# One decay-zero scan over both channel tiles in the first chunks of a Mamba, attention and expert kernel

## The chip, the cores and the metric

The kernel runs on one core of one Trainium2 chip. The metric is the device time of one launch in microseconds. Before the change the median of three runs is 3574.44 us (3572.05 to 3581.58). Engine names: PE is the matrix engine, DVE the vector engine, ACT the scalar engine with the activation tables, POOL the general engine that here issues accumulating transfers and small copies, SP the engine that only issues transfers.

## The reference

Eight samples of 256 channels by 1024 tokens go through two layers. The first layer is a Mamba block and a feed-forward block, the second is attention over the 1024 tokens of a sample and a mixture of experts. The change touches only the scan of the Mamba block:

```python
def step(h, inputs):
    dt_t, B_t, C_t, x_t = inputs
    dA = jnp.exp(dt_t[..., None] * A)
    h = dA * h + (dt_t * x_t)[..., None] * B_t[:, None, :]
    y = jnp.einsum('bds,bs->bd', h, C_t)
    return (h, y)
...
h0 = jnp.zeros((B, d_inner, d_state), x.dtype)
_, ys = jax.lax.scan(step, h0, seq)
```

There are 512 inner channels (`d_inner`) and 16 states (`d_state`), so a sample has 512 x 16 recurrences of 1024 tokens, each of which starts at zero. All is in float32.

## The kernel before

**Tiles.** Channels lie on the 128 partitions, tokens along the free dimension. The 512 inner channels are four tiles of 128; two tiles form a half (`h` is 0 or 1, and `q` is the tile within it). A sample is cut into two chunks of 512 tokens, so there are 16 chunks, numbered from 0. An even chunk is the first of its sample and starts from the state zero; an odd one is the second and starts from what the first left in `state`.

**A step.** A chunk has 32 steps, one for each state `s` and half `h`; a global step number is `g`. A step does this:

- `decay(g, q)`, L595, on ACT: `da = exp(dt * -A)` for the tile `q`, 128 x 512, into one of four rotating buffers `da`.
- `inputs(g)`, L605, on DVE: `hb = xd * B`, 128 x 1024, both tiles of the half in one instruction. `B` and `C` come as `bc`, which SP loads ahead.
- `scan(g, q)`, L616, on DVE: the recurrence along 512 tokens, in place in `hb[:, q, :]`, one instruction for each tile. Its start value is the constant 0 in an even chunk and a column of `state` in an odd one. In an even chunk, after the second scan, POOL copies the last column of both tiles to `state` (L629).
- `sums(g)`, L631, on DVE: `hb = hb * C`, in place; then POOL issues a transfer that adds `hb` to the chunk's accumulator `dx` (L639).

**The loop** (L1688 to L1715) goes over all 512 steps. For each it emits scan 0, then decay 0 of the step two ahead, scan 1, then decay 1 of the step two ahead, the inputs of the next step, and this step's sums. The decay of two steps ahead takes the buffer that the scan just emitted has read.

**What else is woven in.** After every one of these DVE instructions `advance()` (L1607) runs. It holds a clock of its own, kept by costs written into the kernel (L104 to L115: a scan is charged 0.16 us and 2.08 ns for each column, other vector work 0.16 us and 1.04 ns), and emits the pieces of other streams that the clock says are ready: the prologue of the next chunk (`prologue`, L462: normalization, projection, convolution, `dt`), the gate (`gate_part`, L642), the epilogue of the chunk before (`epilogue`, L674: output projection and feed-forward), attention (L1075) and the experts (L1298). Urgencies are at L1588. Attention of a sample runs in 32 units, each of four score matmuls, exponentials on ACT, and eight sums on PE. Where the clock finds PE idle, `keep_warm` (L1593) emits a matmul with zero weights (`warm`, or into an open attention sum, `num`). So the order of the instructions on each engine is fixed when the kernel is built, and the clock decides it. The prologue of chunk i + 1 starts at the step `FRONT[i]` of chunk i (L252), the gate at `GATE[i]` (L253). The prologue ends with the products of `xm` and `dt` (L574), for which the accumulating transfers into `dt` must have landed; the steps of the next chunk can't begin before (L1700).

**The end.** After the last step the last chunk's epilogue, the attention of the last sample and its experts remain, with what is left of the sample before.

Nearly all instructions are recorded at one line (L100, or L95 for transfers), since a helper issues them; in the views they are told apart by the names of their tiles.

Of the kernel before, what the change touches and what calls it, by code (L numbers as in the profile page):

```python
# [9 lines left out]
F32 = mybir.dt.float32  # L10
BF16 = mybir.dt.bfloat16
I32 = mybir.dt.int32
AF = mybir.ActivationFunctionType
ALU = mybir.AluOpType
# [3 lines left out]
P = 128  # L18
B, C, L = 8, 256, 1024
KC = C // P  # L20
CH = 512
NCH = L // CH
# [6 lines left out]
NSTEP = NHALF * NS  # L29
# [25 lines left out]
def hybrid_kernel(ctx: ExitStack, tc: tile.TileContext, a: dict, out: bass.AP):  # L55
# [6 lines left out]
    class Model:  # L62
# [3 lines left out]
        t = end = moved = 0.0  # L66
# [50 lines left out]
    act, vec = Queue(nc.scalar, act_cost), Queue(nc.vector, vec_cost)  # L117
# [51 lines left out]
    zero_c = const.tile([P, 1], F32, name="zero_c")  # L169
# [12 lines left out]
    neg_a = const.tile([P, ND * NS], F32, name="neg_a")  # L182
# [21 lines left out]
    state = const.tile([P, NS, ND], F32, name="state")  # L204
# [255 lines left out]
    chunk = {}  # L460
# [119 lines left out]
    das, bcs, hbs = {}, {}, {}  # L580

    def load_bc(n):
        i, s = divmod(n, NS)
        bc = work_pool.tile([P, 2, CH], F32, name=f"bc_{n}", tag="bc", bufs=AHEAD + 1)
        landed = sp.dma_start(
            bc, chunk[i]["bc_d"][s].partition_broadcast(P)
        )
        bcs[n] = (bc, landed)

    def place(g):  # L590
        i, k = divmod(g, NSTEP)
        s, h = divmod(k, NHALF)
        return i, s, h

    def decay(g, q):  # L595
        i, s, h = place(g)
        da = work_pool.tile([P, CH], F32, name=f"da_{g}_{q}", tag="da", bufs=4)
        n = (2 * h + q) * NS + s
        act.activation(da, chunk[i]["dt"][h][:, q, :], AF.Exp, scale=neg_a[:, n : n + 1])
        das[g, q] = (da, act.at)  # L600
        if q and s == NS - 1:
            model.end = act.at
            t4.put(chunk[i]["dt"][h])

    def inputs(g):  # L605

        i, s, h = place(g)
        hb = hbs[g] = h4.now(f"hb_{g}")
        bc, landed = bcs[g // NHALF]
        vec.at = max(vec.at, landed)  # L610
        xd = chunk[i]["xd"][h]
        vec.tensor_tensor(hb, xd, bc[:, 0, :].unsqueeze(1).to_broadcast([P, 2, CH]), ALU.mult)
        if s == NS - 1:
            t4.put(xd)

    def scan(g, q):  # L616

        i, s, h = place(g)
        c = i % NCH
        hb = hbs[g]  # L620
        d = 2 * h + q
        da, done = das.pop((g, q))
        vec.at = max(vec.at, done)
        vec.tensor_tensor_scan(
            hb[:, q, :], da, hb[:, q, :], 0.0 if c == 0 else state[:, s, d : d + 1],
            ALU.mult, ALU.add,
        )
        if q and c < NCH - 1:
            pool.tensor_copy(state[:, s, 2 * h : 2 * h + 2], hb[:, :, CH - 1])  # L629

    def sums(g):  # L631

        i, s, h = place(g)
        me = chunk[i]
        bc, _ = bcs[g // NHALF] if h < NHALF - 1 else bcs.pop(g // NHALF)
        hb = hbs.pop(g)
        vec.tensor_tensor(hb, hb, bc[:, 1, :].unsqueeze(1).to_broadcast([P, 2, CH]), ALU.mult)
        model.t = vec.at
        me["landed", h] = pool.dma_start(out=me["acc", h], in_=hb, accum_op=ALU.add)  # L639
        h4.put(hb, at=me["landed", h])  # L640

    def gate_part(i):  # L642

        me = chunk[i]
        mem = Owner(t4, 3, 2)
        xn = yield from mem.take(f"xz_{i}")
        yield sp.dma_start(xn, me["xn_d"])
        sz, ps = [], None
        for d in range(ND + 1):
            if d:  # L650
                h, q = divmod(d - 1, 2)
                act.activation(
                    sz[h][:, q, :], ps, AF.Identity, bias=b_in[:, ND + d - 1 : ND + d]
                )
                banks.put(ps)
            if d < ND:
                if d % 2 == 0:
                    sz.append((yield from mem.take(f"sz_{i}_{d // 2}")))
                ps = yield from banks.take(f"z_{i}_{d}")
                for k in range(KC):  # L660
                    pe.matmul(
                        ps, w_in[:, k, DI + d * P : DI + (d + 1) * P], xn[:, k, :],
                        start=(k == 0), stop=(k == KC - 1),
                    )
                yield
        mem.put(xn)
        for t in sz:
            act.activation(t, t, AF.Silu)
        lnexp()
        mem.end()  # L670
        yield
        me["sz"] = sz
# [887 lines left out]
    with tc.tile_pool(name="work", bufs=1) as work_pool:  # L1560

        def tagged(tag, n):
            return Slots(
                lambda nm, k: work_pool.tile([P, 2, CH], F32, name=nm, tag=f"{tag}_{k}"), n
            )

        t4, h4, pt4 = tagged("t4", T4), tagged("h4", H4), tagged("pt", PT)
        for b in range(B):
            for m, nm in ((x1_d, "x1_d"), (t_d, "t_d"), (xf_d, "xf_d")):
                m[b] = dram.tile([NCH, P, KC, CH], F32, name=f"{nm}_{b}", tag=f"{nm}_{b}")  # L1570
# [16 lines left out]
        due, done = [], set()  # L1587
        URGENT = {"a": 0, "p": 1, "g": 2, "e": 2, "o": 3, "s": 4, "x": 5, "y": 5}  # L1588

        def start(stream, key, at=0.0):  # L1590
            due.append([at, URGENT[key[0]], len(done) + len(due), stream, key])
# [15 lines left out]
        def advance():  # L1607


            while True:  # L1610
                model.t = min(model.t + TICK, vec.at)
                for d in sorted(due, key=lambda d: d[1:3]):
                    while d in due and d[0] <= model.t + 0.05:
                        if d[1] > 2 and max(pe.at, act.at) > model.t + LAG:
                            break
                        model.end = model.t
                        try:
                            at = next(d[3])
                        except StopIteration:
                            due.remove(d)  # L1620
                            done.add(d[4])
                            break
                        if at == POLL:
                            break
                        d[0] = (model.end if at is None else at) + 0.1
                keep_warm()
                if model.t >= vec.at:
                    break

        def idle(t):  # L1630

            vec.at += t
            advance()
# [48 lines left out]
        nsteps = B * NCH * NSTEP  # L1682
        for n in range(AHEAD):
            load_bc(n)
        for n in range(4):
            decay(n // 2, n % 2)
        inputs(0)
        for now in range(nsteps):  # L1688
            i, k = divmod(now, NSTEP)
            if i + 1 < B * NCH and k == FRONT[i]:  # L1690
                start(prologue(i + 1), ("p", i + 1), model.t)
            if k == GATE[i]:
                start(gate_part(i), ("g", i), model.t)
            n = now // NHALF + AHEAD
            if now % NHALF == 0 and n < B * NCH * NS:
                while "bc_d" not in chunk.get(n // NS, {}):
                    idle(0.5)
                load_bc(n)
            if now + 2 < nsteps:
                while "dt" not in chunk.get((now + 2) // NSTEP, {}):  # L1700
                    idle(0.5)
            for q in range(2):
                scan(now, q)
                advance()
                if now + 2 < nsteps:
                    decay(now + 2, q)
            if now + 1 < nsteps:
                while not h4.free:
                    idle(0.5)
                inputs(now + 1)  # L1710
                advance()
            sums(now)
            if k == NSTEP - 1:
                start(epilogue(i), ("e", i), model.t)
            advance()  # L1715
# [13 lines left out]
    with tc.If(large != 0):  # L1729
# [21 lines left out]
        with tc.tile_pool(name="moe", bufs=1) as pl:  # L1751
# [99 lines left out]
            for b in range(B):  # L1851
# [8 lines left out]
                hb = pl.tile([P, 2, NF], F32, name=f"hb_{b}", tag="mhb", bufs=2)  # L1860
# [24 lines left out]
                for c in range(NCH):  # L1885
                    tok = slice(c * CH, (c + 1) * CH)
                    n = f"{b}_{c}"
                    h = pl.tile([P, 2, NF, CH], F32, name=f"mh_{n}", tag="mh", bufs=2)
# [9 lines left out]
                    r = pl.tile([P, KC, CH], F32, name=f"mr_{n}", tag="mr", bufs=2)  # L1898
# [80 lines left out]
```

## Time and profile before

| | |
|---|---|
| median of the runs | 3574.44 us |
| the profiled execution | 3582.58 us, its span 3580.8 us |
| scans with start value 0 (even chunks) | 512, mean 1210 ns |
| scans with a start value from `state` (odd chunks) | 512, mean 1269 ns |
| products `hb<-xm,bc` and `hb<-hb,bc` | 512 each, mean 1204 and 1221 ns |
| decays on ACT | 1024, mean 718 ns |
| copies of the last column on POOL | 256, mean 900 ns |
| granted clock of PE | 0.949 on average |

The page gives each engine's busy time, the span in 40 slices with a digit for tenths, the chain of work that ended last, and groups of instructions. A group's line has its engine, operation, tiles (out, then in), shapes, count, busy time in us and mean length in ns, then the idle time of the engine just before them and what ended it. The recorded lengths of neighbours on one engine can overlap: their sum is more than the time from the first start to the last end. A view in stretches gives, for each of a list of windows, the busy time of each engine in us with the number of instructions; PEclk is the granted clock.

### The profile page before, as it was taken

Reading aid. Unit: us, or ns where it says so; the run is one execution under the profiler, and the core shown is the slowest. Engines: PE = TensorE matmul, PEld = TensorE weight load, DVE = VectorE, ACT = ScalarE, POOL = GpSimd, SP = SyncE. Lnnn points to the kernel's source line nnn. Section 1 sums busy time; section 2 is a strip of 40 time slices with the busy share of each in tenths; the row PEclk is TensorE's granted clock in tenths of the full one; section 3 lists DMA queues with packets and bytes.
Section 4 is the critical chain, followed back from the end, with each engine's and each line's share of the span. In section 5 each row is a group of like instructions: output and inputs, shape, how many; then the busy total and the mean of one; then the engine's idle time right before and its main releaser. Section 6 shows DMA issues by size and latency. Waiting matters only on the chain.

```text
span 3580.8 us, 40009 instructions
## 1 busy us (share of the span) xinstructions
PE 3235.4 (90%) x14383; PEld 1419.1 (40%) x14383; DVE 3023.1 (84%) x3308; ACT 2468.9 (69%) x3539; POOL 947.5 (26%) x1052
## 2 busy tenths in 40 slices
PE   8876859998999999999999999898999999999997
PEld 5544344333443334343433344333434343335334
DVE  4879999999999999999999999989999999971021
ACT  4463737686687866797778777796778777854644
POOL 0233123312342224322331234223332233211010
PEclk9778989999999999999999999999999999999999
DMA  4667787778788878987787878897788878861120
GB/s 119 162 139 169 175 180 176 165 176 191 193 195 205 181 167 201 209 197 177 189 206 169 207 191 196 186 206 165 175 206 177 197 196 189 204 139 65 38 72 16
DMA packets 187329, 605.66 MB, mean 169 GB/s; under 512 B 25440, under 2 KB 36320, under 8 KB 187120
## 3 DMA queue, kind: packets, MB, share of 16 engines
q0 software_dynamic: 103392, 364.44, 52.4%
q1 hardware_dynamic: 83728, 238.57, 20.6%
q8 instruction: 115, 1.88, 0.2%
q14 instruction: 94, 0.77, 0.1%
HBM read 238.55 MB, written 62.39 MB: 84 GB/s over the span
## 4 chain that ended last, share of the span: by engine, by line
PE 36%; DVE 33%; issue 11%; ACT 7%; DMA 7%; POOL 5%; POOLq 0%; DVEq 0%; SPq 0%; ACTq 0%
DVE hb L100 25%; PE re L100 4%; PE he L100 3%; POOL state L100 3%; PE num L100 3%; PE sc L100 3%; PE warm L100 3%; PE fh L100 3%; DVE xm L100 3%; DMA dx<-hb 2%; PE facc L100 2%; PE den L100 2%; PE qkp L100 2%; ACT L100 2%; DMA dt<-u 2%
## 5 line engine op out<-in xcount | busy, mean ns | idle before, releaser
L100 ACT ACTIVATE da<-dt,neg_a 128x512 f32<-128x512 f32 x1024 | 720.1, 718 | 486.8 <-DVE hb L100 471.0
L95 POOL DMA_DIRECT2D dx<-hb x512 | 442.8, 867 | 1618.4 <-DVE hb L100 1351.2
L100 DVE TENSOR_TENSOR hb<-hb,bc 128x1024 f32<-128x1024 f32 x512 | 625.2, 1221 | 51.5 <-POOL state L100 20.8
L100 DVE TENSOR_TENSOR_SCAN hb<-da,state,hb 128x512 f32<-128x512 f32 x512 | 632.7, 1269 | 7.7 <-ACT da L100 7.7
L100 DVE TENSOR_TENSOR hb<-xm,bc 128x1024 f32<-128x1024 f32 x512 | 616.5, 1204 | 8.1 <-DMA dx<-hb 8.0
L100 DVE TENSOR_TENSOR_SCAN hb<-da,hb 128x512 f32<-128x512 f32 x512 | 603.0, 1210 | 1.0 <-ACT da L100 0.9
L100 ACT ACTIVATE pt<-sc 128x1024 f32<-128x1024 f32 x512 | 493.8, 1016 | 99.2 <-PE sc L100 98.9
L100 PE MATMUL warm<-mean_c,zero_c 128*128 128x256 f32 x1398 | 417.3, 427 | 46.9 <-ACT dt L100 10.0
L100 PE MATMUL sc<-qk,qk 32*128 32x512 f32 x2048 | 344.4, 652 | 24.0 <-ACT pt L100 17.9
L100 POOL COPY state<-hb 128x2 f32<-128x2 f32 x256 | 230.3, 900 | 436.7 <-DVE hb L100 424.6
L100 PEld LDWEIGHTS warm<-mean_c,zero_c 128*128 128x128 f32 x1398 | 263.4, 205 | 207.1 <-PE warm L100 78.1
L100 PE MATMUL num<-pt,v 128*32 128x512 f32 x2048 | 282.4, 621 | 41.1 <-DVE ot L100 40.9
L100 PE MATMUL den<-pt,ecb 128*32 128x512 f32 x2048 | 277.3, 610 | 0.0
L100 PE MATMUL facc<-fh,w 128*128 128x512 f32 x512 | 231.5, 600 | 4.9 <-ACT re L100 2.8
L100 PE MATMUL fh<-x_f,w 128*128 128x512 f32 x480 | 227.2, 606 | 3.0 <-DVE xn L100 1.7
L100 PE MATMUL he<-xe,g 128*128 128x512 f32 x448 | 217.5, 613 | 5.9 <-ACT xp L100 3.7
L100 ACT ACT_TABLE_LOAD x169 | 216.8, 1283 | 7.6 <-PE var_a L100 4.0
L100 PE MATMUL re<-he,g 128*128 128x512 f32 x472 | 217.0, 607 | 2.6 <-ACT pt L100 2.1
L100 PEld LDWEIGHTS sc<-qk,qk 32*128 32x128 f32 x2048 | 105.7, 186 | 216.0 <-ACT pt L100 108.2
L100 PE MATMUL mo<-sz,w_out 128*128 128x512 f32 x256 | 120.9, 616 | 55.9 <-DVE sz L100 55.9
L100 DVE SCALAR_TENSOR_TENSOR xm<-xp,vecs,xm 128x512 f32<-128x512 f32 x192 | 143.3, 747 | 8.4 <-ACT xm L100 3.9
L100 PEld LDWEIGHTS facc<-fh,w 128*128 128x128 f32 x512 | 95.6, 191 | 125.0 <-issue 114.4
(349 smaller groups left out, 4107.9 us busy)
## 6 DMA issues: line engine op xcount, KB each, us to landing
dx<-hb POOLq DMA_DIRECT2D x512, 512.0 KB
bc<-bc_d SPq DMA_DIRECT2D x256, 512.0 KB
dt<-e POOLq DMA_DIRECT2D x32, 512.0 KB
dt<-u POOLq DMA_DIRECT2D x32, 512.0 KB
xe<-xf_d SPq DMA_DIRECT2D x28, 512.0 KB
xn<-in_x SPq DMA_DIRECT2D x16, 512.0 KB
xn_d<-xn SPq DMA_DIRECT2D x16, 512.0 KB
xz<-xn_d SPq DMA_DIRECT2D x16, 512.0 KB
```

What stands on the lines that cost most here:

```text
L95: f(*args, **kw)
L100: return f(*args, **kw)
```

## The change

In even chunks one scan now covers both tiles of the half: 1024 columns, the first tile's 512 tokens and then the second's. For the second tile's recurrence to start at zero, the decay at its first token is zero. Three things go with it:

- The four rotating decay buffers become one tile `da_all`, 2 (step parity) x 2 (tile) x 512, so that both tiles' decays are adjacent.
- For the second tile in even chunks the decay leaves out the first column and computes 511. The zero is written there by a copy on ACT, for the first two steps of each even chunk only (one for each parity); nothing overwrites it until the next odd chunk.
- In even chunks both decays of the step two ahead are emitted after the wide scan. In odd chunks the order is as it was.

```diff
     def decay(g, q):
         i, s, h = place(g)
-        da = work_pool.tile([P, CH], F32, name=f"da_{g}_{q}", tag="da", bufs=4)
+        da = da_all[:, g % 2, q, :]
         n = (2 * h + q) * NS + s
-        act.activation(da, chunk[i]["dt"][h][:, q, :], AF.Exp, scale=neg_a[:, n : n + 1])
-        das[g, q] = (da, act.at)
+        skip = 1 if q and i % NCH == 0 else 0
+        if skip and g % NSTEP < 2:
+            act.copy(da[:, :1], zero_c)
+        act.activation(
+            da[:, skip:], chunk[i]["dt"][h][:, q, skip:], AF.Exp, scale=neg_a[:, n : n + 1]
+        )
+        das[g, q] = act.at
...
-        da, done = das.pop((g, q))
+        done = das.pop((g, q))
         vec.at = max(vec.at, done)
-        vec.tensor_tensor_scan(
-            hb[:, q, :], da, hb[:, q, :], 0.0 if c == 0 else state[:, s, d : d + 1],
-            ALU.mult, ALU.add,
-        )
+        if c == 0:
+            if q:
+                both = hb.rearrange("p a t -> p (a t)")
+                vec.tensor_tensor_scan(
+                    both, da_all[:, g % 2].rearrange("p a t -> p (a t)"), both, 0.0,
+                    ALU.mult, ALU.add,
+                )
+        else:
+            vec.tensor_tensor_scan(
+                hb[:, q, :], da_all[:, g % 2, q, :], hb[:, q, :], state[:, s, d : d + 1],
+                ALU.mult, ALU.add,
+            )
...
+        da_all = work_pool.tile([P, 2, 2, CH], F32, name="da_all", tag="da")
...
                 scan(now, q)
                 advance()
-                if now + 2 < nsteps:
-                    decay(now + 2, q)
+                if now + 2 < nsteps and (q or i % NCH):
+                    for r in range(0 if i % NCH == 0 else q, q + 1):
+                        decay(now + 2, r)
```

## The prediction

> **What bounds the kernel now.** I read the page's busy shares, then the 40 slices, the costliest groups, the waits of DVE, the busy time in stretches cut at each chunk's first scan, and last the timelines of DVE in a first chunk and of PE at the end.
>
> ```profile
> PE 3235.4 (90%) x14383; PEld 1419.1 (40%) x14383; DVE 3023.1 (84%) x3308; ACT 2468.9 (69%) x3539; POOL 947.5 (26%) x1052
> ...
> PE   8876859998999999999999999898999999999997
> ...
> DVE  4879999999999999999999999989999999971021
> ...
> PE 36%; DVE 33%; issue 11%; ACT 7%; DMA 7%; POOL 5%; POOLq 0%; DVEq 0%; SPq 0%; ACTq 0%
> ...
> L100 DVE TENSOR_TENSOR_SCAN hb<-da,state,hb 128x512 f32<-128x512 f32 x512 | 632.7, 1269 | 7.7 <-ACT da L100 7.7
> ...
> L100 DVE TENSOR_TENSOR_SCAN hb<-da,hb 128x512 f32<-128x512 f32 x512 | 603.0, 1210 | 1.0 <-ACT da L100 0.9
> L100 ACT ACTIVATE pt<-sc 128x1024 f32<-128x1024 f32 x512 | 493.8, 1016 | 99.2 <-PE sc L100 98.9
> L100 PE MATMUL warm<-mean_c,zero_c 128*128 128x256 f32 x1398 | 417.3, 427 | 46.9 <-ACT dt L100 10.0
> ```
>
> Two engines are full at once. DVE is at nine tenths until slice 36 and then nearly empty; PE stays full for the rest. So there are two regimes: the scan stretch (first scan at 93 us, last one over at 3186 us, by the scans' own records) and a tail of 395 us in which PE works alone. The second scan group is the one the change touches: 512 scans of 512 columns whose start value is the constant 0. Before them DVE waits for a decay 1.0 us in all, so they are bound by DVE itself.
>
> ```profile
> core 0: us, PE busy (x) PEld busy (x) DVE busy (x) ACT busy (x) POOL busy (x), PEclk, DMA share, GB/s
> ...
> 865.00:1063.00 198.00, 179.80 (x580) 82.14 (x580) 183.07 (x208) 135.38 (x194) 77.79 (x84) 0.97 0.84 194
> 1063.00:1249.00 186.00, 173.28 (x885) 67.45 (x883) 181.03 (x175) 151.25 (x213) 38.33 (x44) 0.97 0.87 194
> ...
> 3186.00:3581.00 395.00, 365.62 (x1749) 159.59 (x1748) 66.50 (x159) 188.33 (x238) 30.21 (x32) 0.98 0.17 47
> ```
>
> The first two rows are a first chunk (of sample 2) and the second chunk behind it: DVE busy 92 and 97%, PE 91 and 93%. The last is the tail: PE 93%, DVE 17%.
>
> ```profile
> 549.81 2.33 DVE L100 TENSOR_TENSOR_SCAN hb<-da,hb 128x512 f32<-128x512 f32 x2
> 552.06 1.20 DVE L100 TENSOR_TENSOR hb<-xm,bc 128x1024 f32<-128x1024 f32 x1
> 553.34 1.23 DVE L100 TENSOR_TENSOR hb<-hb,bc 128x1024 f32<-128x1024 f32 x1
> 554.48 0.28 DVE L100 SCALAR_TENSOR_TENSOR sq_a<-var_a,sq_a 128x128 f32<-128x128 f32 x1
> ```
>
> A step of a first chunk: from the pair's start to the next start is 552.06 - 549.81 = 2.25 us. The recorded lengths (1.21 each) overlap, so starts count, not lengths. By the single records the second scan starts 1.134 us after the first, and the product behind it 1.116 us after the second.
>
> [...] No run yet shows a scan of 1024 columns.
>
> **Part by part.**
>
> *256 pairs become 256 scans.* The streaming stays; one fixed term per pair goes. [...] Bounds: [...] if the wide scan streams no better than the pair, 0. All eight first chunks hold these, and DVE has no cover there.
>
> *The wide scan waits for both decays.* Before, half q's decay was needed only by scan q. Both are now issued behind the wide scan, since they overwrite buffers that it reads. Room: from its end to the scan two steps on lie four products and a scan, 4 x 1.12 + 2.2 = 6.7 us, against two decays of 0.72. What is queued on ACT ahead can be a Gelu block (four of about 1 us and two table loads of 1.28 us: 6.6 us), which just about fits. Cost: 0 taken, at most 1 us for three blocks in each of 8 chunks, 24 us. Behind a late scan stand the products, POOL's state copy and its DMA.
>
> *ACT.* 256 decays of 511 columns instead of 512, with an odd first word: nothing by the row (0.72 us at either length)[...]. 16 copies of one column at 0.18 us (the row of copies of three columns): 3 us on ACT, hidden. POOL's state copies and all DMA issues are as many as before; they follow the scan as before, and nothing is moved past SP's queue.
>
> *The order.* The planner in the kernel charges each merged pair 0.16 us less, so everything that it weaves between the steps moves. In the emitted order of both programs I weighted PE's matmuls with their spacing in the trace (0.86 us for a full 512-column product, 3.15 us for an attention unit of 4 scores and 8 sums):
>
> - Before the last scan PE has 18 us less real work, ACT about 14 us less, DVE 9 small instructions less (about 4 us).
> - Behind the last scan stand 42 attention units instead of 37, and 20 small normalization matmuls more. The trace fits: 292 score records / 8 = 36.5 units lie behind the last scan.
> - The second chunks get heavier: chunks 5 and 7 each take 14 us more PE work, the first chunks before them less.
> - 70 more keep-warm matmuls (821 to 891) are emitted.
> - The last product of the prologues of chunks 5, 11 and 13 moves from step 29 to steps 26, 26 and 27 of the chunk before. That relieves a wait for the landing of dt, 2.3 us at 1052 us (chunk 5's).
>
> ```profile
> 3189.18 1.37 PE L100 MATMUL sc<-qk,qk 32*128 32x512 f32 x8
> 3190.48 1.07 PE L100 MATMUL num<-pt,v 128*32 128x512 f32 x8
> 3191.36 1.04 PE L100 MATMUL den<-pt,ecb 128*32 128x512 f32 x8
> 3192.34 1.20 PE L100 MATMUL sc<-qk,qk 32*128 32x512 f32 x8
> ```
>
> These are units in the tail, 3.16 us apart with no gap: five more cost 16 us unless they fill holes. From 3186 to 3400 us PE is idle or warming only about 15 us, and the new order emits as many warm matmuls there, so I let them fill nothing; the small matmuls add 1 to 2 us.
>
> *Sum.* Scan stretch: -17 (merge) - 4 (moved DVE work) - 2 (dt) = -23 us. Tail: +17 us. Net -6 us. The profiled execution took 3582.58 us (span 3580.8 and 1.8 around it), 8.1 above the median of the runs, 3574.44; I put the difference on the median: 3568 us.
>
> **Rivals.**
>
> *A, the likeliest (0.50):* the scans' gain arrives and the tail takes most of it back: 3568, between 3558 and 3580 by the bounds above. For it: both engines are full, and PE's real work is unchanged. What isn't saved in PE's holes isn't saved.
>
> *B, the tail pays little (0.25):* the five units fill PE's waits in the last epilogue (9 us warm, 2 idle between 3186 and 3285), and the second chunks carry their added PE work in their own holes (20 to 26 us each). Then -23 + 5 = -18: 3556. Against it: the unchanged count of warm matmuls.
>
> *C, second chunks run over (0.20):* in them the last prologue product stays at step 29, so the next chunk's scans wait for it, and PE gets up to 14 us more ahead of it. Chunk 7 has 170 us of real PE work (its matmul records less the warm ones) in 193; with 184 it would be at 95%, above the 93% that the fullest stretch reaches. If the prologue ends 5 us late in each of the five chunks 5, 7, 9, 11 and 13: +25 - 6 = +19: 3593. It decides once the waits for dt in these chunks, 2 to 4 us now where there are any, grow by more than 3 us each. The 70 added warm matmuls, 0.43 us each, 30 us of PE time, speak for holes of this kind.
>
> *D, no saving (0.05):* the wide scan takes as long as the pair: +17 on A's sum, 3585.
>
> **How the numbers follow.** A measurement of this kernel can tell about 0.3%, 11 us, from no change: under 3563.7 is faster, over 3585.2 slower. A gives faster 0.17, same 0.32, slower 0.01; B faster 0.23, same 0.02; C slower 0.20; D same 0.02, slower 0.03. Sum: faster 0.40, same 0.36, slower 0.24. The range takes B's middle and C's: 3548 to 3593. A's own is 3558 to 3580.
>
> **What would show it.** A group of 256 scans of 1024 columns, 2.26 to 2.28 us by record and 2.18 to 2.20 us from start to start: the merge's step. Start to start of 2.25: D. Last scan's end some 20 us earlier and a tail of about 410 us: A; a tail of under 402: B. Waits for dt or for prologue steps that grow in odd chunks, and a stretch no shorter than before: C. DVE's wait for decays above 10 us in the new group would make the decay step wrong. I am wrong altogether if the end moves by more than 25 us either way.

## The result, and the profile after

The changed kernel takes 3631.35 us (median of four runs, 3625.80 to 3634.05). Before, in the same comparison, it is 3573.24 us (four runs, 3567.18 to 3581.58). The ratio of the means is 1.0159, with a 95% interval of 1.0134 to 1.0184: the change makes the kernel 1.6% slower, and the time lies above the range of the prediction. The profiled execution took 3625.80 us with a span of 3624.0, 43.2 us more than the span of before.

The page of the changed kernel, first the busy shares, then the rows of PE and DVE over 40 slices, then three groups (busy us, mean ns | idle before):

```profile
PE 3276.6 (90%) x14523; PEld 1444.1 (40%) x14523; DVE 3008.8 (83%) x3052; ACT 2464.3 (68%) x3555; POOL 939.8 (26%) x1052
...
PE   8866959998889999999899999999999998999997
...
DVE  4979999999999899998999999979999799951021
...
L100 DVE TENSOR_TENSOR_SCAN hb<-da_all,state,hb 128x512 f32<-128x512 f32 x512 | 631.3, 1270 | 2.3 <-ACT da_all L100 2.3
...
L100 DVE TENSOR_TENSOR_SCAN hb<-da_all,hb 128x1024 f32<-128x1024 f32 x256 | 584.7, 2284 | 2.1 <-ACT da_all L100 2.1
...
L100 PE MATMUL warm<-mean_c,zero_c 128*128 128x256 f32 x1482 | 450.3, 432 | 35.6 <-ACT dt L100 9.0
```

The change does what it says: 256 scans of 1024 columns stand where 512 of 512 stood, and DVE waits for their decays 2.1 us in all. DVE is busy 14.3 us less than before (3023.1 to 3008.8), yet the span is longer. PE is busy 41 us more, but without the matmuls of zero weights its work is about the same (2777 us before, 2774 after): the rest is keep-warm work, 84 more of these records in the group above and 140 more in all, 1690 to 1830. A matmul leaves two records here (the four score matmuls of a unit stand as `x8` in the timelines), so these are 70 matmuls more. Neither engine got more of the reference's work to do: DVE waits more, and PE fills more time with zero weights.

The wide scan itself in DVE's timeline (start, length, instruction), at the place shown of before:

```profile
554.64 1.22 DVE L100 TENSOR_TENSOR hb<-hb,bc 128x1024 f32<-128x1024 f32 x1
555.78 2.29 DVE L100 TENSOR_TENSOR_SCAN hb<-da_all,hb 128x1024 f32<-128x1024 f32 x1
557.98 1.20 DVE L100 TENSOR_TENSOR hb<-xm,bc 128x1024 f32<-128x1024 f32 x1
```

From its start to the next start are 557.98 - 555.78 = 2.20 us, against 2.25 for the pair. Over the 161 such cases in the trace the mean is 2.201: 49 ns saved, 256 x 0.049 = 12.5 us.

**Where the 43 us are.** I cut the DVE records of both traces at the first scan of each chunk, and summed the idle time ahead of each instruction. "Work" is the stretch from the first scan to the end of the last, less these waits. The last column is experiment 6, which comes below.

| us | before | after | experiment 6 |
|---|---|---|---|
| first scan | 93.3 | 96.3 | 96.5 |
| DVE's work in the stretch | 2911.8 | 2889.4 | 2886.1 |
| DVE's waits in even chunks | 107.7 | 107.3 | 109.7 |
| DVE's waits in odd chunks | 73.6 | 114.2 | 67.8 |
| tail | 394.3 | 416.8 | 417.0 |
| span | 3580.8 | 3624.0 | 3577.1 |

DVE does 22.4 us less in the stretch, 12.5 of it by the merge; the rest moved out of it. Then it waits 40.5 us more in the odd chunks, whose steps the change leaves as they were, and the tail is 22.5 us longer. Of the waits in odd chunks, those ahead of the prologue's instructions (`xm`, `e`, `xn`, `sq_a`, `xp`) grow from 14.5 to 40.7 us, and those ahead of other streams' instructions from 43.3 to 67.5; those ahead of the steps' own shrink from 15.8 to 5.9. Sorted by what ended them (waits over 0.15 us), those for ACT grow most, from 21.5 to 50.9 us; those for PE grow from 26.8 to 36.6 and those for transfers from 19.9 to 22.1. By chunk the prologue's waits are:

| odd chunk | 1 | 3 | 5 | 7 | 9 | 11 | 13 | 15 |
|---|---|---|---|---|---|---|---|---|
| before, us | 0.3 | 0.4 | 2.4 | 3.9 | 0.4 | 1.0 | 6.0 | 0 |
| after, us | 0.3 | 0.5 | 9.6 | 10.5 | 6.3 | 3.4 | 10.1 | 0 |

The busy time by stretch of the changed kernel, for chunks 4, 5 and 7 and the tail (the columns' names are in the first line):

```profile
core 0: us, PE busy (x) PEld busy (x) DVE busy (x) ACT busy (x) POOL busy (x), PEclk, DMA share, GB/s
868.00:1068.00 200.00, 170.07 (x508) 80.33 (x500) 180.59 (x175) 123.89 (x183) 76.59 (x83) 0.92 0.80 187
1068.00:1265.00 197.00, 186.91 (x946) 71.90 (x942) 181.24 (x175) 161.40 (x227) 39.15 (x45) 0.97 0.84 187
...
1458.00:1666.00 208.00, 201.35 (x962) 78.23 (x960) 181.25 (x174) 170.01 (x237) 49.81 (x51) 0.98 0.81 185
3207.00:3624.00 417.00, 382.48 (x1888) 165.59 (x1884) 70.68 (x168) 200.37 (x254) 31.03 (x33) 0.98 0.18 49
```

and chunk 7 before:

```profile
1444.00:1637.00 193.00, 184.20 (x898) 72.44 (x894) 181.42 (x174) 158.34 (x222) 50.50 (x52) 1.00 0.89 202
```

Chunk 5 had 186 us before with the same 181 us of DVE work; now it takes 197, so DVE's share falls from 97 to 92%. Chunk 7 grew from 193 to 208 us, and PE is busy 97% of it, 95% before. In chunk 4 PE is busy less than before (170 against 180 us), and the chunk is no shorter. So PE's load went from a first chunk, which gained nothing by it, into second chunks that were nearly full. Without the matmuls of zero weights PE is busy 862 us of the five odd chunks from 5 to 13 before and 900 after; together these chunks last 978 us before and 1005 after.

The end of chunk 7 shows one prologue that runs late, here with a wait for a transfer; it is the longest of its kind, not the commonest kind. First before, the last `e` and the two products `xm<-xm,dt` that close the prologue, from DVE's timeline:

```profile
1599.40 1.21 DVE L100 SCALAR_TENSOR_TENSOR e<-u,e 128x1024 f32<-128x1024 f32 x1
...
1615.99 1.22 DVE L100 TENSOR_TENSOR xm<-xm,dt 128x1024 f32<-128x1024 f32 x1
...
1625.71 1.23 DVE L100 TENSOR_TENSOR xm<-xm,dt 128x1024 f32<-128x1024 f32 x1 [3.59 <-DMA dt<-u]
```

and the same place after:

```profile
1636.89 1.22 DVE L100 TENSOR_TENSOR tn_t<-tn_t,var_t 128x1024 f32<-128x1024 f32 x1 [3.74 <-PE var_t L100]
...
1640.09 1.22 DVE L100 SCALAR_TENSOR_TENSOR e<-u,e 128x1024 f32<-128x1024 f32 x1
1649.10 1.23 DVE L100 TENSOR_TENSOR xm<-xm,dt 128x1024 f32<-128x1024 f32 x1 [7.79 <-DMA dt<-u]
```

Between `e` and the first product lie 16 DVE instructions before, and none after. Behind this `e` POOL still has to issue the last transfers into `dt`, and these must land before the products. Before, 16.6 us lay from the start of `e` to that of the first product, filled with other work of DVE; now `e` comes when the chunk's steps are used up, and the next instruction is the one that waits, 7.79 us. At the ends of chunks 5, 9 and 13 the instructions between fall from 12 to 4, from 20 to 12 and from 17 to 3; at that of chunk 11 they rise from 5 to 8.

The tail, in PE's timeline of the changed kernel:

```profile
3217.95 1.14 PE L100 MATMUL sc<-qk,qk 32*128 32x512 f32 x8
3222.11 1.06 PE L100 MATMUL num<-pt,v 128*32 128x512 f32 x8 [3.02 <-DVE ot L100]
3222.97 1.07 PE L100 MATMUL den<-pt,ecb 128*32 128x512 f32 x8
3223.97 1.14 PE L100 MATMUL sc<-qk,qk 32*128 32x512 f32 x8
...
3226.89 3.70 PE L100 MATMUL mo<-sz,w_out 128*128 128x512 f32 x8
```

The attention units stand among the epilogue's matmuls (`mo`), with a hole of 3.02 us for a result of DVE. Behind the last scan 320 score records lie now, 292 before: 40 units against 36.5. In windows that begin at the last scan PE is busy 382.5 us of 417 now and 364.6 of 393 before: 18 us more busy time, about 5 of it zero weights (46 to 51 us), and 6 us more idle.

### The profile page after: what moved, and what is told of

It reads as the page before. It is cut to its first block, busy times and chain, and to the rows that moved or that the text cites. A ratio compares the mean times of both kernels' runs of the same rounds, so it can differ in the third digit from the quotient of the medians.

```text
span 3624.0 us, 40014 instructions
## 1 busy us (share of the span) xinstructions
PE 3276.6 (90%) x14523; PEld 1444.1 (40%) x14523; DVE 3008.8 (83%) x3052; ACT 2464.3 (68%) x3555; POOL 939.8 (26%) x1052
## 5 line engine op out<-in xcount | busy, mean ns | idle before, releaser
L100 ACT ACTIVATE da_all<-dt,neg_a 128x512 f32<-128x512 f32 (+1 forms) x1024 | 699.4, 716 | 485.9 <-DVE hb L100 477.0
L100 DVE TENSOR_TENSOR_SCAN hb<-da_all,state,hb 128x512 f32<-128x512 f32 x512 | 631.3, 1270 | 2.3 <-ACT da_all L100 2.3
L100 DVE TENSOR_TENSOR_SCAN hb<-da_all,hb 128x1024 f32<-128x1024 f32 x256 | 584.7, 2284 | 2.1 <-ACT da_all L100 2.1
L100 PE MATMUL warm<-mean_c,zero_c 128*128 128x256 f32 x1482 | 450.3, 432 | 35.6 <-ACT dt L100 9.0
L100 PEld LDWEIGHTS warm<-mean_c,zero_c 128*128 128x128 f32 x1482 | 282.4, 207 | 219.0 <-PE warm L100 91.6
L100 PE MATMUL sc<-qk,qk 32*128 32x512 f32 x2048 | 342.7, 649 | 22.8 <-ACT pt L100 8.2
L100 POOL COPY state<-hb 128x2 f32<-128x2 f32 x256 | 212.5, 830 | 352.2 <-DVE hb L100 323.3
L100 PE MATMUL he<-xe,g 128*128 128x512 f32 x448 | 229.1, 639 | 6.4 <-ACT he L100 5.7
L100 PEld LDWEIGHTS facc<-fh,w 128*128 128x128 f32 x512 | 94.8, 190 | 125.9 <-issue 115.0
```

Of the source, the lines that this page charges most:

```text
L100: return f(*args, **kw)
```

## The experiments

All kernels compute the whole reference. The order on each engine is fixed when the kernel is built, by the kernel's own clock; so the instruction and the order can be had apart: emit another instruction while the clock is charged as it was, or charge the clock otherwise and leave the instructions alone. Ratios are of means to the kernel before on the same chip in the same comparison, with 95% intervals, so they need not equal the quotient of the medians to the last digit.

| experiment | order on PE | scans in even chunks | FRONT, GATE | median us | ratio |
|---|---|---|---|---|---|
| 1 | of before | wide, at the second scan's place | old | 3601.24 | 1.0044 [1.0021, 1.0068] |
| 2 | of the change | two, back to back | old | 3639.03 | 1.0154 [1.0132, 1.0177] |
| 3 | redrawn | wide | old | 3610.99 | 1.0090 [1.0066, 1.0114] |
| 4 | redrawn | two, as before | old | 3618.10 | 1.0099 [1.0074, 1.0124] |
| 5 | redrawn | two, as before | old | 3615.76 | 1.0097 [1.0080, 1.0114] |
| 6 | redrawn | wide | chosen anew | 3578.26 | 0.9995 [0.9985, 1.0005] |
| 7 | of before | wide, at the first scan's place | old | 3586.02 | 1.0013 [1.0004, 1.0022] |
| 8 | of before | two, at the second scan's place | old | 3600.59 | 1.0049 [1.0032, 1.0066] |
| 9 | redrawn | two, as before | chosen anew | 3572.22 | 0.9982 [0.9973, 0.9992] |
| 10 | of 6 | two, back to back | as in 6 | 3587.79 | 1.0024 [1.0009, 1.0038] |
| 11 | of 9 | wide, at the first scan's place | as in 9 | 3583.79 | 1.0013 [1.0003, 1.0022] |
| 12 | of before | two, as before; decays in pairs | old | 3579.62 | 1.0012 [0.9999, 1.0025] |
| 13 | redrawn | wide | searched longer | 3569.37 | 0.9981 [0.9970, 0.9991] |

My theory after the result was that the redrawn order costs the time, by late prologues in odd chunks and a longer tail. The rival was the instruction: the wide scan holds back the decays, the sums or the state copies.

**1. The wide scan in the order of before.** The clock is charged as before, at the old places; the wide scan is emitted where the second scan stood, and both decays behind it. PE, POOL and SP have the order of before. The edit against the kernel before, in parts:

```diff
+        if c == 0:
+            model.do(vec, vec_cost("tensor_tensor_scan", hb[:, q, :]))
+            if q:
+                both = hb.rearrange("p a t -> p (a t)")
+                nc.vector.tensor_tensor_scan(
...
+                    if i % NCH == 0:
+                        decay(now + 2, q, put=False)
+                        if q:
+                            for r in range(2):
+                                decay(now + 2, r, plan=False)
```

> The clock in the kernel is charged as before the change (two scans, two decays, each where it was), so PE, POOL and SP have the order of before to the last instruction; DVE runs the wide scans and ACT the paired decays of the change. Order theory (the 58 us come from the new order): the wide scan saves 49 ns a pair, 12 us, so about 3561 us, ratio 0.996. Instruction theory (the wide scan's wait for both decays, or the decays in pairs, costs the time): 3600 to 3630.

1.0044: most of the 1.6% is gone, so the order is most of it. But it is no gain: 0.8% above what the order theory had. The prologue's waits in odd chunks are back at 12.1 us and the tail at 393.8.

**2. The order of the change without the wide scan.** The clock is charged for the wide scan; two scans are emitted.

```diff
+                model.do(vec, vec_cost("tensor_tensor_scan", both))
+                for r in range(2):
+                    nc.vector.tensor_tensor_scan(
+                        hb[:, r, :], da_all[:, g % 2, r, :], hb[:, r, :], 0.0,
...
```

> The order of the change on every engine, but each wide scan is issued as two scans of 512 back to back. Order theory: as slow as the change or slower by the 12 us, 3630 to 3645. Instruction theory: 3575 to 3600.

1.0154, and the change 1.0159: not told apart, although DVE has 12.3 us more work in it. The loss needs no wide scan. In this order no gain by the width shows at the end; the intervals leave room for about 10 us at most.

**3. The charge of the pair kept.** The change, with the wide scan charged as much as the pair was.

```diff
+                vec.at += 0.16
                 vec.tensor_tensor_scan(
...
```

> The change, but the clock charges the wide scan 2.45 us, as much as two scans, instead of 2.29. If the smaller charge is what makes the new order bad, the time falls to 3560 to 3580. If the order is bad because both decays and the clock's step now come in one piece, it stays at 3615 to 3635. The instruction theory expects 3600 to 3635 too.

1.0090: somewhat over half of the loss stays, between what either theory had. Where the scan and the decays stand in the emission redraws the order too, not only the charge.

**4 and 5. Before, with other charges.** The instructions of before, all of them; in even chunks the clock gets 0.08 us less for each scan (4, what the change takes off per scan) or 0.08 us more (5).

```diff
+        if c == 0:
+            vec.at -= 0.08
```

> The kernel before, unchanged in its instructions, but the clock charges each scan of an even chunk 0.08 us less, 0.16 a pair as in the change. If the smaller charge alone makes the order bad: 3610 to 3650. If not: 3565 to 3585. Instruction theory: 3573.

> The kernel before, unchanged in its instructions, but the clock charges each scan of an even chunk 0.08 us more, the opposite of the run with 0.08 less. Theory of the ill-fitting order (FRONT and GATE fit one order alone, so that any other is worse, in whichever direction the charge moves): 3600 to 3640, ratio 1.006 to 1.016. Theory of the charge that is too small (the clock runs ahead of the chip, so a larger charge helps or does nothing): 3555 to 3580.

1.0099 and 1.0097. With the same instructions, a charge moved either way by 0.08 us costs 1%. So it is not only that a smaller charge makes the clock too hasty: with the start steps `FRONT` and `GATE` as they were, the redrawn order is worse in either direction. What runs late differs. In both profiles the tail is 20 us longer or more (416.3 us in 4, 414.3 in 5), and DVE's waits in the stretch grow by 19 and 17 us. In 4 they grow in the odd chunks (73.6 to 94.8 us), in 5 in the even ones (107.7 to 129.7), while its odd chunks wait less than before (68.9). DVE's waits in chunk 11 of experiment 5 (us in total, times, longest):

```profile
DVE e L100 <- ACT u L100: 16.3, 2, 14.7
DVE tn_t L100 <- PE mu_t L100: 5.9, 1, 5.9
DVE xm L100 <- ACT dx L100: 4.0, 1, 4.0
```

A step of the prologue waits 14.7 us at once for `u` from ACT, and the chunk takes 220 us instead of 208.

**6. The change with start steps of its own.** `FRONT` and `GATE` were chosen by a search that kept the steps for which the kernel's own clock ended earliest; nothing measured went into it.

```diff
-    FRONT = (5, 6, 6, 4, 8, 9, 6, 8, 8, 0, 10, 8, 10, 8, 9)
-    GATE = (15, 17, 14, 15, 17, 13, 22, 16, 16, 22, 16, 14, 16, 21, 17, 17)
+    FRONT = (5, 6, 5, 6, 8, 10, 2, 8, 9, 0, 8, 6, 9, 2, 10)
+    GATE = (15, 17, 15, 15, 15, 23, 22, 15, 10, 20, 16, 12, 24, 21, 17, 24)
```

> The change, with FRONT and GATE chosen anew for its own charges (so that the clock in the kernel ends earliest, from the old values by single steps); nothing else differs. Ill-fitting order: most of the 58 us come back, 3565 to 3600. If the cost lies in the instructions (wide scan, paired decays): 3615 to 3640.

0.9995: the whole loss is won back. In chunk 7 DVE again has work between `e` and the first product:

```profile
1621.72 1.23 DVE L100 SCALAR_TENSOR_TENSOR e<-u,e 128x1024 f32<-128x1024 f32 x1 [0.63 <-ACT u L100]
...
1627.98 1.21 DVE L100 TENSOR_TENSOR tn_t<-fo,mu_t 128x1024 f32<-128x1024 f32 x1
...
1636.73 1.23 DVE L100 TENSOR_TENSOR xm<-xm,dt 128x1024 f32<-128x1024 f32 x1 [2.30 <-DMA dt<-u]
```

Eight instructions stand between, and the wait is 2.30 us, not 7.79. By the table above, DVE's waits in odd chunks fall from 114.2 to 67.8 us, those for ACT from 50.9 to 19.8. Most of that is in other streams' instructions (67.5 to 30.9); the prologue's own waits only fall from 40.7 to 30.3. So late prologues alone are not the loss: this order bears 30 us of them. At the end of its chunk 5, 12 instructions stand between `e` and the first product as in the kernel before, and DVE still waits 9.5 us for both products (4.0 for ACT, 5.6 for a transfer): the number of instructions doesn't decide alone. PE's work in that chunk, without zero weights, is still that of the change (175 us, before 160). Over the odd chunks from 5 to 13 it is back at 858 us, in 962 us of time. The tail stays long, at 417.0.

**7 and 8. The instruction in the order of before, again.** Experiment 7 puts the wide scan at the first scan's place, with the decays at their old places; 8 is experiment 1 with two scans.

```diff
-            if q:
+            if q == 0:
```

> Order of before on PE, ACT, POOL and SP, and the wide scan at the place of the first of the two scans on DVE, where the first try with the old order had it at the place of the second and the decays in pairs behind it. If the 0.4% of that try came from other streams' DVE work that now stood ahead of all of the scan (DVE waits for it 1.1 us too early) or from the decays in pairs: 3560 to 3580, ratio 0.995 to 1.000. If the wide scan costs by itself (ACT's first decay waits for its end, the last consumers of DVE's other work come 1.1 us later): 3590 to 3610.

> The first try with the old order, but with two scans of 512 back to back at the place of the second, and the decays in pairs behind them. If the wide scan's 12 us arrive in that try and the placement costs 28: 3605 to 3615, ratio 1.008. If the saving of width doesn't arrive at the end at all: 3595 to 3605, ratio 1.004. If the width itself did harm: 3570 to 3580.

Experiment 8 is about as slow as 1 (1.0049 against 1.0044), so the 0.4% there needs no wide scan. Experiment 7 is 0.13% slower than before, though DVE has 13.8 us less work in its stretch by the same reckoning: the waits grew by 24. ACT's timeline in its chunk 2 shows one of them:

```profile
556.30 0.67 ACT L100 ACTIVATE fh<-fh,b 128x512 f32<-128x512 f32 x1
559.28 0.72 ACT L612 ACTIVATE da_all<-dt,neg_a 128x512 f32<-128x512 f32 x1 [2.31 <-DVE hb L639]
559.91 0.67 ACT L100 ACTIVATE fh<-fh,b 128x512 f32<-128x512 f32 x1
```

The decay overwrites what the wide scan reads, so it waits for all of it, 2.31 us, and the feed-forward's `fh` stands behind it.

**9. Control: before with start steps chosen anew.**

```diff
+    FRONT = (0, 3, 6, 2, 10, 1, 7, 1, 9, 3, 9, 9, 11, 6, 9)
+    GATE = (15, 15, 19, 19, 17, 9, 10, 19, 16, 25, 16, 18, 16, 22, 17, 15)
```

> Control: the kernel before with FRONT and GATE chosen anew in the same manner, nothing else changed. If the old values were a good fit on the chip already, 3560 to 3585; if the refit of the change won back its time only because any search helps any kernel by as much, this one gains as much, 3520 to 3550.

0.9982. The search also gains a little on the kernel before, so experiment 6 must be held against this one too, and then the change is 0.13% behind, with intervals that overlap.

**10 and 11. The width in the orders chosen anew.** Experiment 10 is 6 with two scans, 11 is 9 with the wide scan at the first scan's place. The edits are those of 2 and 7.

> The refitted change, with each wide scan issued as two scans of 512 back to back; all other instructions in the same order. If DVE's 12 us count at the end once the order fits: 12 us above the refitted change, 3590, ratio 1.003. If they become waits, as in the other two orders: within 5 us of it.

> The refitted kernel before, with the wide scan at the place of the first scan (everything on PE, ACT, POOL and SP in the order of the refitted kernel before). If the 12 us count: 12 us below it. If they become waits: within 5 us of it. This or the control is the candidate that beats both kernels.

Experiment 10 lies 0.29% above 6, about 10 us, and the intervals don't overlap: in that order most of the width's 12.5 us reaches the end. Experiment 11 lies 0.31% above 9, about 11 us: in that one the wide scan costs. The profiles' scan groups, first of experiment 6, then of 11, differ in the waits for decays only by 2.9 us:

```profile
L100 DVE TENSOR_TENSOR_SCAN hb<-da_all,hb 128x1024 f32<-128x1024 f32 x256 | 584.8, 2284 | 0.0
```

```profile
L639 DVE TENSOR_TENSOR_SCAN hb<-da_all,hb 128x1024 f32<-128x1024 f32 x256 | 584.7, 2284 | 3.0 <-ACT da_all L612 2.9
```

**12. Only the decays in pairs.** Experiment 8 with each scan at its own place.

```diff
-            if q:
-                for r in range(2):
+            nc.vector.tensor_tensor_scan(
+                hb[:, q, :], da_all[:, g % 2, q, :], hb[:, q, :], 0.0,
...
```

> Order of before on PE, DVE, POOL and SP with the two scans of 512 each at its own place; only ACT differs: both decays of an even chunk's step are issued behind the second scan (the second of 511 columns). If the 0.4 to 0.5% of the first try with the old order come from the decays in pairs: ratio 1.004 to 1.005. If they come from the place of the scan on DVE, behind other streams' work: 0.999 to 1.001.

1.0012, up to 1.0025: pairing the decays costs a quarter of a per cent at most. The rest of experiment 8's 0.49% is then the place of the first scan on DVE. With it moved back, other streams' instructions in even chunks wait 68.7 us in 8 and 46.7 in 12 (before 44.2): whatever stood between the two scans comes up 1.1 us sooner and finds its input not there yet. That last clause is my reading of these waits, not an experiment of its own.

**13. The change, searched longer.** The edit is that of experiment 6 with other numbers.

```diff
+    FRONT = (5, 6, 5, 6, 11, 1, 2, 7, 9, 0, 8, 6, 9, 3, 10)
+    GATE = (15, 21, 15, 15, 15, 23, 20, 24, 10, 19, 16, 12, 9, 16, 17, 24)
```

> The change with FRONT and GATE fitted longer in the same manner (the clock's own end is 16 us earlier than in the first refit). If the fit of the order is what sets the time, about 10 to 16 us below the first refit: 3560 to 3570, ratio 0.995 to 0.997, which beats both kernels. If the first refit was as good as the chip allows: 0.999 to 1.001.

0.9981: 0.19% faster than before and 1.8% than the change (0.9981 / 1.0159), but no better than the control, 0.9982. With the start steps found for each, both programs end at the same time; the control was not searched longer as this one was. The kernel's clock had promised 16 us against experiment 6; the ratios differ by 0.14%, 5 us.

**What the width is worth.** Each row compares two kernels with the same order on PE. Work and waits are DVE's, from the first scan to the last, reckoned as in the table of the result. In the last two rows the scan's place differs as well.

| wide against two scans | work, us | waits, us | at the end, by ratios |
|---|---|---|---|
| change against 2 | -12.3 | +7.2 | +0.05%, not told apart |
| 1 against 8 | -11.9 | +4.4 | -0.05%, not told apart |
| 6 against 10 | -12.8 | +11.1 | -0.29% |
| 7 against before | -13.8 | +24.2 | +0.13% |
| 11 against 9 | -11.7 | +22.2 | +0.31% |

In the first two rows the intervals leave room for a gain of some 10 and 12 us. DVE's saving is there each time, and in the profiled executions from a third of it to all of it and more turns into waits. For experiments 6 and 10 the runs show a gain of which the two profiles show little within the stretch (1.6 us; their spans differ by 5.9): single executions of one kernel differ by as much (those of experiment 6 lie between 3570.79 and 3588.37 us), so where it arrives stays open.

## Why the prediction failed, point by point

**The bound: right as far as it went.** Two full engines and a tail of PE alone were read rightly. "What isn't saved in PE's holes isn't saved" agrees with experiment 2, where no gain by the width shows, but no run tests it on its own. And "DVE has no cover there" was only half of it: DVE's work sets the pace of even chunks only while what it waits for comes on time (with the same instructions its waits there were 107.7 us before and 129.7 in experiment 5).

**"256 pairs become 256 scans": right in kind, term mis-sized.** Taken were 17 us, 66 ns for each pair, an estimate of mine that no run had shown; measured were 49 ns and 12.5 us. Of the pair's 2250 ns from start to start 2201 stay, so no more than 49 is saved by merging two.

**"The wide scan waits for both decays": right.** Nothing was taken; 2.1 us were measured, with DVE's waits for decays below before in sum (4.4 against 8.7 us over both scan groups).

**ACT: right.** Its busy time fell by 4.6 us; the odd start of the 511 columns cost nothing that shows (709 ns in the mean for these decays, 718 for those of 512), and the 16 copies took 0.19 us each.

**The dt relief: right in its place, wrong as a sum.** The wait of 2.3 us at 1052 us is gone: at the end of chunk 4 both products now go without a wait. But the waits of these products for `dt` together rose from 14.9 to 21.4 us, since others were brought closer to their `e`.

**The tail: right in kind.** +17 was predicted, +22.5 measured. The size is luck in part: by records 3.5 more units lie there, not 5, and of the 18 us by which PE's busy time grew about 5 are zero weights. Added to that are 6 us of idle time, waits such as that for `ot` above.

**The failed step: the sum of the scan stretch, "-17 (merge) - 4 (moved DVE work) - 2 (dt) = -23 us".** As a sum of DVE's work it is nearly right (17 + 4 = 21 us less predicted, 22.4 measured, though as 12.5 by the merge and 10 moved). But it put the growth of DVE's waits at nothing, and they grew by 40 us: the stretch became 17.7 us longer, not 23 shorter. The prediction had named a move of the end by more than 25 us as being wrong altogether; it moved by 58.

What the waits come from was half in its hands. It had the amounts: 14 us more PE work in chunks 5 and 7 each, and the trace has 15 and 17. Case A charged nothing for them. The added waits, most of them for ACT and some for PE, show that the new order did not come free. The prediction never looked at distances, how much other work lies between a producer and its consumer on the engine that will wait, as between `e` and `xm` in chunk 7. Experiment 6 changes both together, so the runs don't tell which of the two counts for more.

Rival C named this, with chunks 5 to 13, and its 25 us fits the prologue's waits (+26.3 over all odd chunks). Still it missed as much again: the instructions of other streams in the odd chunks wait 24 us more, `tn_t<-fo,mu_t` alone 21.6 instead of 9.9 us over the whole run. And its point of decision was badly chosen: the waits for dt grew by over 3 us in only two of these chunks (3.6 to 7.8 us in chunk 7, none to 3.5 in chunk 9); the others lost their time ahead of other prologue steps. The 70 extra matmuls of zero weights were the sign that PE would find holes; they were all in the emitted order, and I counted them for C, but gave it 0.20. One reading in C was wrong: 93% is not what the fullest stretch reaches, chunk 7 itself stood at 95% (184.20 of 193 us, in the line shown above). And the lower end of the range, 3548, lies below B's middle, 3556, which it was said to take; the upper end is the one that was passed.

DVE was busy 92% of a first chunk (183.07 of 198 us in chunk 4 before the change), and that made a wider instruction look like time gained there; in four of the five pairs of the table above no gain shows at the end, and in one about 10 us do.

**What the prediction didn't ask.** Whether the start steps fit the new order. Experiments 4 and 5 show that two other redrawn orders cost 1% each with the old steps, and experiment 6 that new steps give the change's whole loss back. With these, the table of the result reads much like case A: the stretch from first to last scan 29.6 us shorter (predicted 23), the tail 22.8 longer (predicted 17), the span 3.6 us shorter (predicted 6). Case A comes near the change in an order fitted to it, not the change as made; that the terms come so close is luck in part, since the order of experiment 6 is another than the one they were reckoned from.

**Left open.** Shown is that the redrawn order with the old start steps costs the time. Which of its late steps decides was not tried one by one, nor was PE's load in the second chunks changed without the distances. Why the wide scan at the first place costs 5 to 11 us is argued from waits on ACT and DVE, and not shown.

## What to carry to other kernels

In a kernel whose order is fixed ahead by a clock with hand-set start steps, changing one instruction's charge changes the whole schedule: test the instruction in the old order, and the new order with the old instruction, before judging either, and set the start steps anew for both sides of the comparison. When two emitted orders are compared, look at the work between producer and consumer on the engine that waits, beside the work for each engine and stage, and don't put the change of the waits at nothing; here neither count foretells the waits alone. A saving on one of two full engines need not reach the end: here 12 us of DVE's work were worth anything from 10 us gained to 11 us lost, by the order around them and the place of the scan.

## What the hardware showed

- Two scans of 512 columns merged into one of 1024 save 49 ns by starts (2250 to 2201), though the recorded lengths suggest 136 (2 x 1210 - 2284). A recorded length is longer than the distance of starts by 85 ns for the narrow scan (1210 against 1125) and by 83 for the wide one (2284 against 2201), so the pair carries this overlap twice and the wide scan once.
- A decay of exactly zero in the middle of a scan lets a second recurrence begin at zero there, and no cost of it shows: the 1024 columns take 2.15 ns each by starts, the pairs 2.20.
